# Two row maxima of a score burst taken one by one in a fused attention kernel

## The chip, the cores and the metric

The kernel runs on one core of a Trainium2 chip. The metric is the device time of one execution in microseconds (us); the kernel before takes 741.09 us (median of 3 runs, 741.09 to 741.41). In the text PE is TensorE (matmuls), PEld its weight loads, DVE is VectorE, ACT ScalarE, POOL GpSimd and SP the queue that issues most transfers. [...] The kernel holds PSUM, the memory that matmuls write to, as one tile of 128 partitions x 8 banks x 512 fp32 values.

## The reference

```
x: (8, 512, 512) fp32    cond: (8, 512)    16 heads of 32
Q = x @ Wq.T + bq ;  K = x @ Wk.T + bk ;  V = x @ Wv.T + bv
tQ = cond @ Wq.T + bq ;  tK = cond @ Wk.T + bk          # one row per batch
scores = (Q + tQ) @ (K + tK).T / sqrt(32)                # per batch and head, 512 x 512
out = x + softmax(scores) @ V
```

Everything is fp32. Four heads (4 x 32 = 128 columns) of one batch make a group; with 8 batches and 16 heads there are T = 32 groups, numbered t.

## The kernel before

The scores of a group are computed twice, once in each orientation. Once with the queries on the partitions: `row_max` (line 470) issues four matmuls through `row_scores` (line 481), one head each, for one chunk of 128 queries. Each head uses 32 of the array's 128 rows, so the four matmuls run side by side, and each fills one PSUM bank of 128 queries x 512 keys. Such a set of four is called a score burst here. From the four banks DVE takes the negated maximum over the keys (`row_max_of`, line 490, two banks per instruction), and ACT then takes exp(score - maximum) with the row sum as a by-product (`denominators`, line 518). The exponentials of that pass are thrown away, only the sums are kept. The profile shows line 518 as an ACTIVATE and a short ACTIVATION_READ_ACCUMULATOR for each head.

Once with the keys on the partitions: `exponentials` (line 555) first broadcasts the maxima of the group into four banks (line 560), adds the transposed scores to them (line 563), and ACT writes exp of each bank to SBUF (line 574). These tiles are the weights that `times_v` (line 579) multiplies by V.

The main loop over t has four stages for each t, one for each chunk, numbered 0 to 3 here. A stage issues, on PE in this order: the broadcasts of line 560, the transposed scores of line 563, the score burst of line 481 for the next group (`row_max(t + 1, 1)`, `(t + 1, 2)`, `(t + 1, 3)` and `(t + 2, 0)` in stages 0 to 3), and then a filler of its own: a part of the next batch's Q projection in stage 0, weights times V and its division in stage 1 (`weighted`), a part of the K projection in stage 2, a part of the V projection in stage 3. The projections use a seven-product scheme on 2 x 2 blocks; a t with odd number makes the first products of Q and K and a t with even number the other ones, for V it is the other way round. So the loop has eight kinds of stage. They are named E0 to E3 for even t and O0 to O3 for odd t.

The order on every engine is written out by hand. ACT does, in each stage: the four exponentials of line 574, then (O0, O2, E3 only) a copy of a first product (line 426), then the four discarded exponentials of line 518. DVE does the two maxima of line 490, then the sums that end the stage's projection: lines 432, 433 and 414 or 417 where the first products are made, lines 446, 447 and 414 or 417 for the others; in stage 3 a copy of the transposed maxima (line 550) stands between the maxima and these sums; in stage 1 it is a reciprocal (626), for two of four t two combinations of x (321 to 325), and a transpose (629).

All eight banks are in use all the time. A table `TURNS` gives, for each of the eight kinds, the bank of each use: entries 0 to 3 are the banks of the transposed scores (some of which the filler takes over afterwards), entries 4 to 7 those of the score burst. A weight load of a score burst therefore waits until the reader of its bank in the stage before is done: ACT's line 518 for banks that held scores, DVE's lines 414, 417, 447 or 629 for banks that held a product.

`row_max_pair` and `row_max_pairs` do the same as `row_max` for single pairs at the end of the program; the change does not touch them. `row_max` is called with its default pairs everywhere.

Of the kernel before, what the change touches and what calls it, by code (L numbers as in the profile page):

```python
# [12 lines left out]
ALU = mybir.AluOpType  # L13
AX = mybir.AxisListType
# [3 lines left out]
def kernel(  # L18
# [38 lines left out]
    nc = tc.nc  # L57
# [5 lines left out]
    HG = P // HD  # L63
    NP = HG // 2
# [42 lines left out]
    def banks(i, n=1):  # L107

        j = TURNS[turn[0]][i]
        if n == 1:  # L110
            return psum[:, j, :]
        k = TURNS[turn[0]][i + 1]
        return psum[:, j : k + 1 : k - j, :]
# [348 lines left out]
    nmax = {}  # L462
    sums = {}

    def open_max(t):
        if t not in nmax:
            nmax[t] = op.tile([P, NS, HG, 1], F32, tag="nmax", name=f"nmax_{t}", bufs=3)
            sums[t] = op.tile([P, NS, HG, 1], F32, tag="sums", name=f"sums_{t}", bufs=3)

    def row_max(t, qc, prs=range(NP)):  # L470
        if t >= T:
            return
        open_max(t)
        for j in range(HG):
            row_scores(t, qc, j, banks(HG + j))
        for pr in prs:
            row_max_of(t, qc, pr, banks(HG + pr * 2, 2))

    def row_scores(t, qc, j, pt):
        r = slice(j * HD, (j + 1) * HD)  # L480
        nc.tensor.matmul(  # L481
            pt,
            qkT["q", t][r, qc * P : (qc + 1) * P],
            qkT["k", t][r, :],
            start=True,
            stop=True,
        )

    def row_max_of(t, qc, pr, pt):
        nc.vector.tensor_reduce(  # L490
            nmax[t][:, qc, pr * 2 : pr * 2 + 2, 0], pt, AX.X, ALU.max, negate=True
        )
# [255 lines left out]

    turn[0] = 13
    row_max(0, 0)  # L750
    denominators(0, 0)
    project_qk(1, "k", banks(1))
    advance()
    row_max(0, 1)
    first_products("q", 0, 1, lambda: denominators(0, 1), nothing, 0, 1)
    advance()
    row_max(0, 2)
    other_products("q", 0, 1, lambda: denominators(0, 2), nothing, (0, 1))
    first_products("k", 0, 1, nothing, nothing, 3, 2)
# [94 lines left out]
    t = T - 3  # L854
# [36 lines left out]
    t = T - 2  # L891
# [101 lines left out]
```

## Time and profile before

| what | value |
|---|---|
| median of 3 runs | 741.09 us (741.09 to 741.41) |
| the profiled execution, whole | 741.09 us |
| its span, first to last instruction | 739.3 us |
| mean granted TensorE clock | 0.999 |
| PE busy | 730.4 us (99%) |
| ACT busy | 629.4 us (85%) |
| DVE busy | 523.4 us (71%) |
| POOL busy | 166.6 us (23%) |

The span leaves 1.8 us of the time outside it. Busy time counts an engine from the start to the modelled end of its instructions, and matmuls overlap: a busy PE can still be held up. In the tables a group of instructions is one line with its engine, operation, written and read tiles, shapes and count, then its busy time and the mean duration of one, then the engine's idle time before them and what ended it. In a timeline a row merges instructions of one line: start, time to the last end, count. Each fp32 matmul is two instructions in the trace, so a score burst is x8.

### The profile page before, as it was taken

Reading aid. Unit: us, or ns where it says so; the run is one execution under the profiler, and the core shown is the slowest. Engines: PE = TensorE matmul, PEld = TensorE weight load, DVE = VectorE, ACT = ScalarE, POOL = GpSimd, SP = SyncE. Lnnn points to the kernel's source line nnn. Section 1 sums busy time; section 2 is a strip of 40 time slices with the busy share of each in tenths; the row PEclk is TensorE's granted clock in tenths of the full one; section 3 lists DMA queues with packets and bytes.
Section 4 is the critical chain, followed back from the end, with each engine's and each line's share of the span. In section 5 each row is a group of like instructions: output and inputs, shape, how many; then the busy total and the mean of one; then the engine's idle time right before and its main releaser. Section 6 shows DMA issues by size and latency. Waiting matters only on the chain.

```text
span 739.3 us, 14941 instructions
## 1 busy us (share of the span) xinstructions
PE 730.4 (99%) x5434; PEld 407.5 (55%) x5434; DVE 523.4 (71%) x727; ACT 629.4 (85%) x1567; POOL 166.6 (23%) x270
## 2 busy tenths in 40 slices
PE   9999999999999999999999999999999999999997
PEld 5576555665555665555565555566555566555332
DVE  3588677777777776687766867777767777667664
ACT  2469889898998988989988988989889898898965
POOL 3721211222211222221122221122221122221130
PEclk9999999999999999999999999999999999999999
DMA  8512212222212222211212221222110111110111
GB/s 265 81 20 39 37 23 44 33 41 44 43 23 37 42 31 44 44 29 31 44 30 44 43 34 26 43 33 41 31 27 9 25 29 30 29 30 12 32 31 29
DMA packets 184765, 29.63 MB, mean 40 GB/s; under 512 B 178410, under 2 KB 182506, under 8 KB 184692
## 3 DMA queue, kind: packets, MB, share of 16 engines
q1 hardware_dynamic: 184112, 28.01, 22.0%
q8 instruction: 42, 0.69, 0.4%
q10 hardware_dynamic: 580, 0.68, 0.3%
q14 instruction: 31, 0.25, 0.1%
HBM read 20.27 MB, written 8.39 MB: 39 GB/s over the span
## 4 chain that ended last, share of the span: by engine, by line
PE 97%; ACT 1%; DMA 1%; DVE 1%; issue 0%; SPq 0%; DVEq 0%; ACTq 0%
PE psum L394 26%; PE psum L481 16%; PE psum L579 16%; PE psum L563 15%; PE psum L391 14%; PE psum L560 6%; PE psum L338 2%; PE psum L544 1%; DMA w_k<-in_L_cond_Wk_dram 1%; ACT e L574 1%; PE psum L254 1%; PE psum L638 0%; PE psum L589 0%; PE psum L677 0%; PE psum L618 0%
## 5 line engine op out<-in xcount | busy, mean ns | idle before, releaser
L490 DVE TENSOR_REDUCE nmax<-psum 128x2 f32<-128x1024 f32 x256 | 301.8, 1220 | 158.1 <-PE psum L481 156.6
L518 ACT ACTIVATE dead<-psum,nmax 128x512 f32<-128x512 f32 x496 | 334.8, 690 | 20.9 <-DVE nmax L490 17.6
L574 ACT ACTIVATE e<-psum 128x512 f32<-128x512 f32 x512 | 264.3, 602 | 59.6 <-PE psum L563 59.4
L481 PE MATMUL psum<-kT,qT 32*128 32x512 f32 x1024 | 142.0, 605 | 0.1
L563 PE MATMUL psum<-qT,kT 32*128 32x512 f32 x1024 | 132.4, 588 | 0.0
L630 POOL TENSOR_TENSOR res<-res,recs 128x512 f32<-128x512 f32 x28 | 29.4, 1049 | 438.5 <-DVE res L629 438.5
L579 PE MATMUL psum<-e,v 128*32 128x512 f32 x1024 | 120.3, 596 | 1.0 <-ACT e L574 0.9
L518 ACT ACTIVATION_READ_ACCUMULATOR dead<-psum,nmax 128x1 f32 x496 | 102.5, 207 | 0.0
L481 PEld LDWEIGHTS psum<-kT,qT 32*128 32x128 f32 x1024 | 58.7, 183 | 60.7 <-ACT dead L518 29.9
L579 PEld LDWEIGHTS psum<-e,v 128*32 128x32 f32 x1024 | 26.8, 110 | 65.9 <-issue 41.1
L560 PE MATMUL psum<-maxT,onesb 3*128 3x512 bf16 x512 | 51.3, 384 | 1.6 <-DVE maxT L550 0.9
L563 PEld LDWEIGHTS psum<-qT,kT 32*128 32x128 f32 x1024 | 51.1, 185 | 2.5 <-issue 0.2
L391 PE MATMUL psum<-wc_v,xc 128*128 128x256 f32 x192 | 49.3, 379 | 0.0
L560 PEld LDWEIGHTS <-onesb 3*128 3x128 bf16 x512 | 13.3, 91 | 60.4 <-issue 51.0
L394 PE MATMUL psum<-xc,wc_q 128*128 128x256 f32 x180 | 46.2, 379 | 0.0
L394 PE MATMUL psum<-xc,wc_k 128*128 128x256 f32 x180 | 46.2, 379 | 0.0
L391 PEld LDWEIGHTS psum<-wc_v,xc 128*128 128x128 f32 x192 | 36.5, 190 | 5.0
L391 PE MATMUL psum<-wT_v,xT 128*128 128x256 f32 x128 | 38.7, 404 | 0.0
L394 PEld LDWEIGHTS psum<-xc,wc_q 128*128 128x128 f32 x180 | 34.2, 190 | 4.7
L394 PEld LDWEIGHTS psum<-xc,wc_k 128*128 128x128 f32 x180 | 34.2, 190 | 4.6
L631 POOL TENSOR_TENSOR res<-res,xr 128x512 f32<-128x512 f32 x28 | 35.7, 1274 | 2.2
L170 POOL TENSOR_TENSOR xr<-xr,bvs 128x512 f32<-128x512 f32 x28 | 35.6, 1271 | 0.2 <-issue 0.2
(157 smaller groups left out, 739.2 us busy)
## 6 DMA issues: line engine op xcount, KB each, us to landing
x<-in_x_dram SPq DMA_DIRECT2D x112, 64.0 KB, 2.4
xr<-in_x_dram SPq DMA_DIRECT2D x112, 64.0 KB, 2.5
out_dram<-res SPq DMA_DIRECT2D x112, 64.0 KB, 2.0
w_q<-in_L_cond_Wq_dram SPq DMA_DIRECT2D x4, 256.0 KB, 4.5
w_k<-in_L_cond_Wk_dram SPq DMA_DIRECT2D x4, 256.0 KB, 3.8
w_v<-in_L_cond_Wv_dram SPq DMA_DIRECT2D x4, 256.0 KB, 4.3
xr<-in_x_dram SPq DMA_DIRECT2D x4, 256.0 KB, 4.0
out_dram<-res SPq DMA_DIRECT2D x3, 256.0 KB, 2.4
```

The lines of the kernel that those rows point to most:

```text
L170: nc.gpsimd.tensor_tensor(xr[t], xr[t], bias, ALU.add)
L391: nc.tensor.matmul(pt, xb, w, start=(kc == kcs[0]), stop=(kc == kcs[-1]))
L394: nc.tensor.matmul(pt, w, xb, start=(kc == kcs[0]), stop=(kc == kcs[-1]))
L481: nc.tensor.matmul(pt, qkT["q", t][r, qc * P : (qc + 1) * P], qkT["k", t][r, :], start=True, stop=True,)
L490: nc.vector.tensor_reduce(nmax[t][:, qc, pr * 2 : pr * 2 + 2, 0], pt, AX.X, ALU.max, negate=True)
L518: nc.scalar.activation(dead, banks(HG + j), AF.Exp, bias=nmax[t][:, qc, j, :], accum_out=sums[t][:, qc, j, :],)
L560: nc.tensor.matmul(bank[j], onesb[r, :], maxT[t][r, :], start=True, stop=False)
L563: nc.tensor.matmul(bank[j], qkT["k", t][r, kc * P : (kc + 1) * P], qkT["q", t][r, :], start=False, stop=True,)
L574: nc.scalar.activation(e[:, i, :], bank[pr * 2 + i], AF.Exp)
L579: nc.tensor.matmul(pt[j * HD : (j + 1) * HD, :], vs[b % 2][:, kc, (g * HG + j) * HD : (g * HG + j + 1) * HD], es[t, kc, j // 2][:, j % 2, ...
L630: nc.gpsimd.tensor_tensor(y, y, rec.broadcast_to([P, NB, BL]), ALU.mult)
L631: nc.gpsimd.tensor_tensor(y, y, xr.pop(t), ALU.add)
```

## The change

In `row_max` the maximum over banks HG and HG + 1 (heads 0 and 1), one instruction over 128 x 1024 values that writes 128 x 2, becomes two instructions over 128 x 512 values that write 128 x 1 each. The pair of heads 2 and 3 is taken as before. The argument `prs`, which no caller passes, is dropped. `row_max` is called for 31 groups and 4 chunks, 124 times; nothing else is edited, and no instruction of another engine is added, removed or moved. The four maxima of a burst stand in `nmax` as before.

```diff
-    def row_max(t, qc, prs=range(NP)):
+    def row_max(t, qc):
         if t >= T:
             return
         open_max(t)
         for j in range(HG):
             row_scores(t, qc, j, banks(HG + j))
-        for pr in prs:
-            row_max_of(t, qc, pr, banks(HG + pr * 2, 2))
+        for j in range(2):
+            nc.vector.tensor_reduce(
+                nmax[t][:, qc, j : j + 1, 0], banks(HG + j), AX.X, ALU.max, negate=True
+            )
+        row_max_of(t, qc, 1, banks(HG + 2, 2))
```

## The prediction

> **What bounds the kernel.** I read the page's busy times and groups first, then the list of waits, then single stages in the timeline. PE is busy throughout, and the chain that ended last is 97% PE, so time can only come from matmuls that are held up while they count as busy.
>
> ```profile
> PE 730.4 (99%) x5434; PEld 407.5 (55%) x5434; DVE 523.4 (71%) x727; ACT 629.4 (85%) x1567; POOL 166.6 (23%) x270
> ...
> L490 DVE TENSOR_REDUCE nmax<-psum 128x2 f32<-128x1024 f32 x256 | 301.8, 1220 | 158.1 <-PE psum L481 156.6
> L518 ACT ACTIVATE dead<-psum,nmax 128x512 f32<-128x512 f32 x496 | 334.8, 690 | 20.9 <-DVE nmax L490 17.6
> ```
>
> DVE's maxima wait for the burst, ACT's discarded exponentials wait 17.6 us in all for the maxima. The list of waits says who holds the burst's weight loads:
>
> ```profile
> PEld psum L481 <- ACT dead L518: 29.9, 77, 0.8
> ...
> ACT dead L518 <- DVE nmax L490: 17.6, 50, 5.0
> ...
> PEld psum L481 <- DVE qT L417: 11.2, 28, 0.9
> ...
> PEld psum L481 <- DVE v L414: 3.4, 14, 0.3
> ```
>
> A late load need not delay a matmul. How much it does is seen in PE's timeline, one pair of t (14, 15), the burst of each stage:
>
> ```profile
> 360.24 1.02 PE L481 MATMUL psum<-kT,qT 32*128 32x512 f32 x8
> ...
> 365.51 1.12 PE L481 MATMUL psum<-kT,qT 32*128 32x512 f32 x8
> ...
> 376.54 1.11 PE L481 MATMUL psum<-kT,qT 32*128 32x512 f32 x8
> ...
> 387.44 1.11 PE L481 MATMUL psum<-kT,qT 32*128 32x512 f32 x8
> ...
> 398.47 1.14 PE L481 MATMUL psum<-kT,qT 32*128 32x512 f32 x8
> ```
>
> E0 (360.24) is undisturbed at 1.02, as are E2, O0 and O2; E1 (365.51), E3, O1 and O3 are stretched. In the trace's single records the step from a burst's first matmul to the filler's first is 954 ns undisturbed, 1,045 in E1, 1,041 in E3, 1,044 in O1 and 1,064 in O3, almost the same in every pair, while every other piece of a stage is constant to 2 ns. So the late loads cost 91 + 87 + 90 + 110 = 378 ns a pair, 5.3 us over 14 pairs. That is the most that this change could give in the loop.
>
> The records also show the rule. Counted from the start of line 563, a burst's first matmuls can start at 862 ns; a head's second load comes 108 ns after its first, and its second matmul 427 ns after that load, but not before 1,290 to 1,301. So a first load is free until about 756 to 765 ns and costs one for one after that. A load follows the release by some 43 to 52 ns.
>
> **The change, part by part.**
>
> *DVE's work.* One reduction of 1024 becomes two of 512. No row shows 512, but the program has a reduction of 128 values from PSUM: 281 ns, against 1,214 for 1024 (1,224 where it waited). The line through them is 1.041 ns per value, which puts 512 at 681 (691). Back to back, DVE starts the next instruction 84 ns before the end of the last: the two reductions of a stage take 2.36 us together, so the second starts 1.14 after the first. The two halves thus occupy 607 + 597 = 1,204 ns instead of 1,141: 63 ns more in each of 124 bursts, 7.8 us of DVE, which has 29% to spare but not everywhere.
>
> *Start.* Today the pair waits for both heads. The trace's semaphore updates show PE's completions posted about 43 ns apart (1,890 and 1,933 after line 563's start in E0), and the reduction starts at 1,957, 24 after the second. Alone, head 0 can start at 1,914. In E0 to E3, O2 and O3 the maxima therefore begin 43 ns sooner. DVE's shift for what follows is s = 63 - 43 = 20 ns.
>
> *ACT.* This is the stage before E1, with the ACT and DVE rows:
>
> ```profile
> 361.34 2.36 DVE L490 TENSOR_REDUCE nmax<-psum 128x2 f32<-128x1024 f32 x2 [1.27 <-PE psum L481]
> ...
> 362.66 0.69 ACT L518 ACTIVATE dead<-psum,nmax 128x512 f32<-128x512 f32 x1 [0.16 <-DVE nmax L490]
> ...
> 363.61 0.41 DVE L446 TENSOR_TENSOR qT<-psum,qT 128x256 f32<-128x256 f32 x1
> ...
> 363.94 0.68 DVE L447 TENSOR_TENSOR qT<-psum,qT 128x512 f32<-128x512 f32 x1
> ...
> 364.58 0.75 DVE L417 SCALAR_TENSOR_TENSOR qT<-psum,tok,qT 128x512 f32<-128x512 f32 x1
> ```
>
> The first maxima end at 361.34 + 1.22 = 362.56, and line 518 starts 95 ns later; ACT issued its last exponential at 361.89 and, at its pitch of 0.48 to 0.49, was free at 362.37. So ACT loses 0.29 us here. After the change head 0's maximum ends at 361.30 + 0.69 = 361.99, and ACT starts at 362.37. Head 1 follows at 363.05. Head 2 waits for the pair, which ends 20 ns later than today: 363.71 + 0.095 = 363.81, against 364.00 now. ACT's last two heads come 190 ns sooner. E1's loads wait for them (the last ends at 798 ns and the load is at 850); at 608 the load is free, and the 88 ns are gone. E1's other gate is DVE's line 417 (load at 737, free until 756), fed by the back-to-back rows 446 and 447. Line 417 waits for PE's last product anyway, with 42 ns to spare over the pitch of 447, so s = 20 costs nothing: **-88 ns in E1**.
>
> E3 has the same relief on ACT, but its first load follows line 417, whose K it needs: 686 ns end, 802 load. Line 417 has the same 42 ns to spare: **0 in E3**. O3 follows O2, where a copy (line 426) keeps ACT until 3,254 ns and the maxima until 3,277: **-22 in O3**. O1 follows O0, where the copy alone sets the start at 3,254: **0 in O1**. E0 waits for line 414, at the end of a back-to-back chain from O3's maxima (2.36 us, then lines 550, 446, 447, 414), load at 736 and 15 ns to spare to the last head: **+5 in E0**. E2 waits for the transpose of line 629, which follows PE's last weighted product; in every other pair two combinations of x before it leave it 74 ns. The earlier PE takes 88 and s takes 20, so it is 34 late, less some 20 of room at the load: **+15 in half of E2**. PE's filler, the wait of line 618 on the second exponential included, has room for E1's 88.
>
> Sum: 14 x (-88 - 22 + 5) = -1.47, E2 +0.10, t = 26 whose E1 is stretched by half only +0.04, the first stages -0.03, the end of the program -0.2 (there the maxima hold ACT for 0.37 and 0.18, and its bursts are stretched by 0.3 and 0.1, of which 0.13 and 0.07 come back). Together -1.6 us, against the profiled execution's 741.09 (739.3 of span and 1.8 around it), which is also the median: **739.5 us**. POOL and the transfers get the maxima of the last chunk 20 ns later; line 544 waits for POOL's end over 1 us later, so nothing follows.
>
> [...] The row says that a second reduction costs 157 ns of fixed time (1,224 less 1,024 values at 1.04), of which 84 are covered: some 63 to 73. [...]
>
> **The rivals.** (a) Forecast, 739.5, own range 738.9 to 740.2. (b) The early start isn't had or the second reduction costs more: s = 40 to 85, E1's relief and the dearer E0 and E3 about cancel. [...] For it: three of four gates of the even stages are DVE chains with 15 to 42 ns to spare. Against: the postings 43 ns apart. (c) Slower: DVE's back-to-back chains become the bound of E0, E1 and E3. [...] For it: PE's slack there is a few tens of ns. Against: the interpolated 63. (d) More: E3's first load is at 802 though its DVE release was at 697; if the rest is ACT's, E3's 87 go too, 14 x 87 = 1.2 us, 738.3. Against: that load needs a separate wait instruction, which the trace shows. That nothing happens isn't a case: three maxima in place of two are issued.
>
> **How the numbers follow.** (a) 0.48, (b) 0.21, (c) 0.19, (d) 0.12. What a measurement can tell from no change is 0.2%, 1.5 us; 739.6 is the line, and six tenths of (a) lie below it. Faster: 0.29 + 0.12 = 0.41. Same: 0.19 + 0.21 = 0.40. Slower: 0.19. The range is 738.3 (d) to 743.0, most of (c).
>
> **What would show it.** 124 reductions of 1024 fewer, 248 of 512 with 680 to 690 ns; DVE's busy time up 8 us; ACT's wait for line 490 from 17.6 to under 8 us; E1's burst at 1.03 instead of 1.12, O3's at 1.12 instead of 1.14, E0's still 1.02. Wrong is the forecast if the halves take over 710 ns, if the first one starts no sooner after the burst, or if E0's or E3's burst grows by more than 0.03.

## The result

The changed kernel takes 739.41 us (median of 13 runs, 739.18 to 740.33) against 741.09 us (13 runs beside it, 740.73 to 742.37): a ratio of 0.9978, 95% interval 0.9969 to 0.9986. The forecast was 739.5. The profiled spans are 737.5 us after and 739.3 before. In the changed kernel lines from `row_max` on have numbers that are higher by 3: the single maxima are line 477, the pair 493, the burst 484, the discarded exponentials 521.

The page of the changed kernel, busy times and groups:

```profile
PE 729.1 (99%) x5434; PEld 406.9 (55%) x5434; DVE 529.9 (72%) x851; ACT 626.4 (85%) x1567; POOL 166.2 (23%) x270
...
L521 ACT ACTIVATE dead<-psum,nmax 128x512 f32<-128x512 f32 x496 | 338.0, 701 | 8.3 <-DVE nmax L477 5.4
...
L477 DVE TENSOR_REDUCE nmax<-psum 128x1 f32<-128x512 f32 x248 | 159.7, 686 | 149.5 <-PE psum L484 149.5
L493 DVE TENSOR_REDUCE nmax<-psum 128x2 f32<-128x1024 f32 x132 | 160.2, 1214 | 2.8 <-PE psum L484 2.8
```

The 248 halves take 686 ns each, and ACT loses 8.3 us ahead of its discarded exponentials where it lost 20.9. Its mean of 701 instead of 690 comes back below. In the list of waits, of the changed kernel (what waits, for what: us in all, times, longest):

```profile
PEld psum L484 <- ACT dead L521: 26.8, 60, 1.0
...
PEld psum L484 <- DVE qT L417: 11.1, 28, 0.5
...
ACT dead L521 <- DVE nmax L477: 5.4, 2, 4.5
...
PEld psum L484 <- DVE v L414: 3.3, 14, 0.2
```

ACT waited 50 times for maxima, 17.6 us in all; it now waits five times, 6.3 us in all (the two of the row, and three for the pair of line 493), all in the first 52 us. The burst's loads wait for ACT 60 times instead of 77, and for DVE as before. DVE's busy time is up by 6.5 us where 8 was named. The timeline of PE, changed kernel, t = 14 and 15, the bursts of E0, E1, E3, O1 and O3:

```profile
359.75 1.03 PE L484 MATMUL psum<-kT,qT 32*128 32x512 f32 x8
...
365.02 1.02 PE L484 MATMUL psum<-kT,qT 32*128 32x512 f32 x8
...
375.96 1.11 PE L484 MATMUL psum<-kT,qT 32*128 32x512 f32 x8
...
386.86 1.20 PE L484 MATMUL psum<-kT,qT 32*128 32x512 f32 x8
...
397.98 1.13 PE L484 MATMUL psum<-kT,qT 32*128 32x512 f32 x8
```

E1's burst has lost its stretch (1.12 to 1.02); E3's and O3's have not. O1's 1.20 is a single stage: in other pairs it is 1.10 to 1.11. It will be explained by the last experiments. DVE and ACT in stage E0, just ahead of E1:

```profile
360.80 1.29 DVE L477 TENSOR_REDUCE nmax<-psum 128x1 f32<-128x512 f32 x2 [1.21 <-PE psum L484]
...
361.86 0.71 ACT L521 ACTIVATE dead<-psum,nmax 128x512 f32<-128x512 f32 x1
362.00 1.21 DVE L493 TENSOR_REDUCE nmax<-psum 128x2 f32<-128x1024 f32 x1
...
364.09 0.75 DVE L417 SCALAR_TENSOR_TENSOR qT<-psum,tok,qT 128x512 f32<-128x512 f32 x1
```

The first maximum starts 1.05 us after the burst's first matmul (before 1.10), and ACT goes on at 361.86 with no idle time in its row, 2.11 us after the burst started (before 2.42). Line 417 still comes 4.34 after the burst, as it did: DVE's longer work cost E1's other gate nothing. In the records of E1 at t = 14, the last two of the heads' first loads started 850 and 856 ns after the start of line 563 (566 now); they now start at 753 and 759, within the 756 to 765 up to which a load is free.

A pair is the eight stages of two successive t. In the single records the whole difference of 1.81 us in span is found: 1.11 in the 13.5 pairs from t = 1 to 27 (43.876 us a pair before, 43.794 after, with stages that are stretched only once left out), 0.30 in such one-off stages (0.76 us before, 0.46 after), 0.13 ahead of t = 1 and 0.30 behind t = 27; the sum is 1.84. Not all of it is the change's. A second execution of the changed kernel starts t = 1 0.09 us later than the first, so the 0.13 is not shown to be an effect. What O1 and O3 give, 11 ns a pair, comes back below.

### The profile page after: what moved, and what is told of

The parts are those of the page before. It is cut to its first block, busy times and chain, and to the rows that moved or that the text cites. A ratio compares the mean times of both kernels' runs of the same rounds, so it can differ in the third digit from the quotient of the medians.

```text
span 737.5 us, 15136 instructions
## 1 busy us (share of the span) xinstructions
PE 729.1 (99%) x5434; PEld 406.9 (55%) x5434; DVE 529.9 (72%) x851; ACT 626.4 (85%) x1567; POOL 166.2 (23%) x270
## 4 chain that ended last, share of the span: by engine, by line
PE 97%; DVE 1%; ACT 1%; DMA 0%; issue 0%; DVEq 0%
PE psum L394 26%; PE psum L582 16%; PE psum L484 15%; PE psum L566 15%; PE psum L391 14%; PE psum L563 6%; PE psum L338 2%; PE psum L547 1%; ACT e L577 1%; PE psum L254 1%; DMA x<-in_x_dram 0%; PE psum L299 0%; PE psum L641 0%; DVE nmax L477 0%; PE psum L592 0%; PE psum L680 0%
## 5 line engine op out<-in xcount | busy, mean ns | idle before, releaser
L477 DVE TENSOR_REDUCE nmax<-psum 128x1 f32<-128x512 f32 x248 | 159.7, 686 | 149.5 <-PE psum L484 149.5
L493 DVE TENSOR_REDUCE nmax<-psum 128x2 f32<-128x1024 f32 x132 | 160.2, 1214 | 2.8 <-PE psum L484 2.8
L484 PE MATMUL psum<-kT,qT 32*128 32x512 f32 x1024 | 140.3, 602 | 0.2 <-DVE kT L417 0.2
L521 ACT ACTIVATION_READ_ACCUMULATOR dead<-psum,nmax 128x1 f32 x496 | 108.6, 219 | 0.0
L484 PEld LDWEIGHTS psum<-kT,qT 32*128 32x128 f32 x1024 | 56.7, 183 | 61.0 <-ACT dead L521 26.8
```

The lines of the kernel that those rows point to most:

```text
L477: nc.vector.tensor_reduce(nmax[t][:, qc, j : j + 1, 0], banks(HG + j), AX.X, ALU.max, negate=True)
L484: nc.tensor.matmul(pt, qkT["q", t][r, qc * P : (qc + 1) * P], qkT["k", t][r, :], start=True, stop=True,)
L493: nc.vector.tensor_reduce(nmax[t][:, qc, pr * 2 : pr * 2 + 2, 0], pt, AX.X, ALU.max, negate=True)
L521: nc.scalar.activation(dead, banks(HG + j), AF.Exp, bias=nmax[t][:, qc, j, :], accum_out=sums[t][:, qc, j, :],)
```

## The experiments

The table has, from the records of each profiled execution, the median step in ns from a burst's first matmul to the filler's first (954 to 956 is undisturbed), and the mean pair in us without stages that are stretched once.

| kernel | E0 | E1 | E2 | E3 | O1 | O3 | pair, us | median, us |
|---|---|---|---|---|---|---|---|---|
| before | 956 | 1046 | 955 | 1041 | 1044 | 1064 | 43.876 | 741.09 |
| changed | 962 | 955 | 965 | 1042 | 1038 | 1059 | 43.794 | 739.41 |
| split in E0 only | 956 | 956 | 956 | 1041 | 1036 | 1058 | 43.778 | 738.93 |
| split in all but E0 | 965 | 1034 | 954 | 1042 | 1037 | 1058 | 43.869 | 740.44 |
| head 1 first | 1008 | 1063 | 956 | 1116 | 1075 | 1071 | 44.113 | 745.11 |
| heads 2, 3 singly | 1008 | 998 | 964 | 1046 | 1038 | 1057 | 43.887 | 740.85 |
| all four singly | 1029 | 956 | 995 | 1056 | 1044 | 1064 | 43.920 | 740.54 |
| split in E0, O2, ends | 956 | 954 | 956 | 1042 | 1044 | 1065 | 43.794 | 739.01 |

Some entries stand between two kinds that alternate from one even t to the next: E2 for the changed kernel (955 and 974), with heads 2, 3 singly (955 and 973) and with all four singly (955 and about 1,038), and E3 for the last two (1,040 and 1,055; 1,041 and 1,071).

### The split in E0 alone, and everywhere else

The edit is to the changed kernel, like the next ones:

```diff
+        single = t % 2 == 1 and qc == 1 and t > 1   # the burst that stage E0 issues
-        for j in range(2):
+        for j in range(2) if single else ():
             nc.vector.tensor_reduce(...)
-        row_max_of(t, qc, 1, banks(HG + 2, 2))
+        for pr in (1,) if single else (0, 1):
+            row_max_of(t, qc, pr, banks(HG + pr * 2, 2))
```

> The maxima of heads 0 and 1 are taken singly in stage E0 alone (14 bursts), together everywhere else. Theory (the gain is ACT's earlier start in E0, which frees the banks that E1's burst loads wait for): E1's step from the burst's first matmul to the filler falls from 1,046 to 955 ns, every other stage stays as before the change (E0 956, E3 1,041, O1 1,044, O3 1,064), E2 goes up by at most 20 in every other pair; 14 x 90 = -1.26, +0.1: 739.9 us, ratio 0.9984. Rival (the gain comes from many stages, or from the maxima starting sooner everywhere): a seventh or less of the change's 1.7 us, 740.8. Rival (the gain is one run's hiccups): E1 stays at 1,046 and the time at 741.1.

Measured: 738.93 us (7 runs), ratio 0.9974, interval 0.9963 to 0.9986. The other way round, the split in all bursts but those (`single = not (t % 2 == 1 and qc == 1)`):

> Heads 0 and 1 singly everywhere but in E0. Theory: E1 stays at 1,046 ns; E0 pays 7 (from O3's maxima), O3 and O1 gain 5 each, E2 has no earlier filler to catch up with, so it stays at 955; the start and the end of the program give 0.25 us. Together about 0.3 us below before: 740.8, ratio 0.9996. Rival (many stages give a little each): most of the 1.7 us stays, 739.6.

Measured: 740.44 us, ratio 0.9994, interval 0.9985 to 1.0003; it is 0.36 below the expected time, and its one-off stretch is 0.06 us where before had 0.76. So 14 of 124 bursts carry all of the gain in the loop: the pair loses 98 ns with them alone, 91 of them in E1, and 7 with all the others. The split of O3's maxima costs E0 its 9 ns (965 against 956). E0 alone was 1.0 us better than expected, of which 0.76 is that this execution has no one-off stretched stage at all.

O1 and O3 read 6 to 8 ns below before in the kernel that leaves their stages alone. In all traces but that of head 1 first they have one of two pairs of values: about 1,037 and 1,058 in six (the changed kernel twice, E0 alone, all but E0, heads 2 and 3, and a kernel below with memsets), 1,044 and 1,064 in seven (before, all four singly, the split in E0, O2 and the ends, and four kernels with memsets, one of them the changed kernel). So these 11 to 13 ns a pair, some 0.15 us in all, go neither with the split nor with its absence. What decides them stays open.

### Head 1 ahead of head 0

```diff
-        for j in range(2):
+        for j in (1, 0):
```

> The two single maxima of the changed kernel in the other order, head 1 and then head 0: the same instructions, but ACT's first discarded exponential needs the second of them. Theory (head 0's earliness is all that is bought): head 0's maximum ends at about 1,957 + 607 + 681 = 3,246 ns after line 563's start, against 3,182 with one instruction for both, so ACT starts 65 later than before the change in E0, E1, O2 and about 87 later in O0; bursts E1 +65, O3 +65, O1 +87 against before, E0 +48 and E3 +21 by VectorE's longer chains: +286 ns a pair, 4.0 us: 745.1, ratio 1.0054. Rival (splitting as such helps, whatever the order): 739.4 to 740.

Measured: 745.11 us (4 runs), ratio 1.0057, interval 1.0043 to 1.0071. The total is as expected, its parts are not: the pair grows by 237 ns and not by 286, E1 by 17 for 65, O1 by 31 for 87, E3 by 75 for 21. The same two instructions as in the changed kernel, and it is slower than before. In its timeline of PE, the bursts of E0, E1 and E3 of t = 14:

```profile
362.05 1.08 PE L484 MATMUL psum<-kT,qT 32*128 32x512 f32 x8
...
367.36 1.22 PE L484 MATMUL psum<-kT,qT 32*128 32x512 f32 x8
...
378.50 1.18 PE L484 MATMUL psum<-kT,qT 32*128 32x512 f32 x8
```

E0 pays here for DVE's second reduction without the early start, with 1,008 ns for 956. The 1.22 in E1 is one-off in this pair; its median is 1,063 ns, above before's 1,046, since in E0 ACT's first discarded exponential starts 71 ns later than before and not 300 sooner. That E1 pays only 17 of the 71 fits E0's own 52, by which E1 begins later; the next experiment shows this. So the gain is the early release of head 0, and the order is what gives it.

### The other pair, and all four, singly

```diff
-        for j in range(2):
+        row_max_of(t, qc, 0, banks(HG, 2))
+        for j in (2, 3):
             nc.vector.tensor_reduce(...)
-        row_max_of(t, qc, 1, banks(HG + 2, 2))
```

> Heads 0 and 1 together as before, heads 2 and 3 one by one: the same added VectorE work, without an earlier head 0. Theory: VectorE's chain is 63 ns later (607 + 597 in place of 1,141), ACT gains nothing; E0 +48, E1 +0 (ACT's late load hides VectorE's), E3 +21, others 0: +69 ns a pair, 1.0 us: 742.1, ratio 1.0013. Rival (VectorE's 63 ns are hidden by its idle quarter): 741.1, no stage changed. Rival (splitting as such helps): 739.5.

Measured: 740.85 us, ratio 0.9997, interval 0.9988 to 1.0006: no slower, where 1.0013 was expected. With all four heads singly (`for j in range(HG)`, no pair):

> All four maxima of a burst singly. ACT gets all four heads in time (head 2 no longer waits for a pair), VectorE's chain is 126 - 43 = 83 ns later than before the change. Theory: E1's gate is now VectorE's line 417, 41 late, so its burst falls only from 1,046 to about 990; E0 +68, E3 +41, O3 -5, E2 +23 on the mean of two: +70 ns a pair, 1.0 us, end of the program -0.1: 742.0, ratio 1.0012; that would show that VectorE's few tens of ns of room are the limit of this kind of change. Rival (more splitting, more relief): below 739.4.

Measured: 740.54 us, ratio 0.9993, interval 0.9984 to 1.0002; 1.0012 was expected. Both came out lower than expected. The timeline of PE of the kernel with heads 2 and 3 singly, E0 and E1 of t = 14:

```profile
360.30 1.08 PE L484 MATMUL psum<-kT,qT 32*128 32x512 f32 x8
365.61 1.07 PE L484 MATMUL psum<-kT,qT 32*128 32x512 f32 x8
```

E0 pays (1,008 ns, +52; +48 was expected), but E1 falls by 48 although nothing releases ACT earlier: its first exponential still starts 3,282 ns after line 566's start, 3,276 before. That start hangs on matmuls ahead of the stall. When E0's burst is stretched by 52, the next stage begins 52 later, and E1's gates stand 52 earlier against it. So a stall in E0 takes the place of the one in E1, and the pair grows by 11 ns, not by 69: 58 ns in each of 14 pairs, 0.8 of the 1.25 us by which the time is below the expected one (13 of the 58 are O1's and O3's). Most of the rest is that its one-off stretched stages come to 0.38 us and not 0.76.

With all four singly E0 pays 73 (68 expected), and E1 is free (956) where DVE's later line 417 was to keep it at 990. E2 pays 80 in half of the pairs, 40 on the mean for 23, and E3 15 on the mean for 41: it pays 30 where E2 is free, and nothing where E2 pays. The pair grows by 44 ns where 70 was expected, 0.4 of the 1.46 us by which the time is below the expected one. Another 0.63 is in one-off stages, 0.1 at the ends of the program; the rest lies between the profiled execution (740.89) and the median.

### The split where it can pay, and the changed kernel beside it

The loops are those of the split in E0 alone; only the choice differs:

```diff
+        single = (
+            (t % 2 == 1 and qc == 1) or (t % 2 == 0 and qc == 3)
+            or t in (0, T - 2) or (t == 1 and qc == 0)
+        )
```

> Heads 0 and 1 singly only where a later burst waits for ACT: E0, O2, and in the first and the last groups. Theory: the change's gain in E1 and O3 and at both ends stays, its costs go: E0 back from 962 to 955, E2 from 975 to 965 in every other pair (the part that the earlier filler causes stays): 14 x 7 + 7 x 10 = 0.17 us below the changed kernel, 739.2 against 739.4, ratio to before 0.9975. Rival (the other splits matter): slower than the changed kernel by 0.2 or more.

> The changed kernel itself, on the same chip as the version that splits only in chosen stages. 739.4, ratio to before 0.9978; E1 955, E0 962, E2 965 on the mean, E3 1,042, O1 1,038, O3 1,059 ns.

Measured: 739.01 us, ratio 0.997, interval 0.996 to 0.9981, against 739.42 us, 0.997 to 0.9988, for the changed kernel on the same chip. O3 reads 1,065 with the maxima of O2 split, for which it waits, just as before (1,064): the gain that was forecast for O3 isn't there. E0 and E2 are back at 956, E2 in every pair, where 965 was expected in every other one.

### The stages that are stretched once

The kernel before has three: t = 11 O0 by 224 ns, t = 22 E1 by 254 and t = 26 E0 by 280. The changed kernel has two, t = 2 E3 by 373 and t = 15 O1 by 88, and a second execution of it has the same two, by 355 and 103. In each, one instruction ahead of it began late. Timeline of DVE, kernel before, ahead of t = 22 E1:

```profile
539.46 0.68 DVE L447 TENSOR_TENSOR qT<-psum,qT 128x512 f32<-128x512 f32 x1
540.46 0.75 DVE L417 SCALAR_TENSOR_TENSOR qT<-psum,tok,qT 128x512 f32<-128x512 f32 x1 [0.31 <-ACT dead L518]
```

Line 417 follows 447 by 0.62 to 0.64 us elsewhere, and by 1.00 here. The row names ACT as releaser, but the records have line 417's separate wait instruction end at 540.06, 0.40 us ahead of it, where 0.05 is usual. The same row in the changed kernel, ahead of t = 2 E3:

```profile
111.28 0.68 DVE L447 TENSOR_TENSOR kT<-psum,kT 128x512 f32<-128x512 f32 x1
112.27 0.75 DVE L417 SCALAR_TENSOR_TENSOR kT<-psum,tok,kT 128x512 f32<-128x512 f32 x1 [0.31 <-DVE kT L447]
```

Counted through DVE's records, the separate wait instructions too, the late ones before are numbers 448, 832 and 960, and this one is 192: all multiples of 64. If the count decides, instructions put ahead of the loop move the stretched stages. The experiment is a few memsets of a column that nobody reads:

```diff
     nc.vector.memset(which, 0.0)
+    pad = const.tile([P, 1], F32, tag="pad", name="pad")
+    for _ in range(4):      # 4, 6 or 5 in the kernel before, 9 in the changed one
+        nc.vector.memset(pad, 0.0)
```

> The kernel before, with four one-element-wide memsets more at the head of DVE's program, long before the loop. Theory: DVE pauses at every 64th of its instructions (separate wait instructions counted; a gap of about 0.48 us where it follows a wait instruction of a chain without idle time), and the kernel before loses 224 + 254 + 280 = 758 ns where this falls into such a chain, in the stages at 293, 540 and 623 us. Four instructions more move every pause four instructions earlier in the program, where by the trace of before none meets line 414, 417 or 490 in a chain of the loop that a burst waits for. Expected: no stage stretched by over 0.1 us in the loop, 740.3 us, ratio 0.999. Rival (the stretched stages come from transfers or from something else fixed in time): the same three stages stretched, 741.1, ratio 1.000.

Measured: 740.41 us, ratio 0.9991, interval 0.9982 to 0.9999. The stretches at t = 11 and t = 22 are gone. At t = 26 E0 one of 203 remains, but from another instruction: number 960 is now the copy of line 550, at the head of the chain to line 414, which I hadn't counted among the chains. DVE ahead of t = 22 E1, with four memsets more (447 and 417 stand in lines 450 and 420):

```profile
539.59 0.68 DVE L450 TENSOR_TENSOR qT<-psum,qT 128x512 f32<-128x512 f32 x1
540.23 0.75 DVE L420 SCALAR_TENSOR_TENSOR qT<-psum,tok,qT 128x512 f32<-128x512 f32 x1
```

Six memsets:

> The kernel before, with six such memsets. Theory: the three pauses leave t = 11, 22 and 26, and others reach line 490 of t = 6 E3 (stage t = 7 O0 stretched by 0.22 us), line 417 of t = 18 E0 (t = 18 E1 by 0.25) and line 414 ahead of t = 24 E0 (by 0.28): 741.1 us, ratio 1.000, but the stretched stages are those. Rival: those of before, t = 11 O0, 22 E1 and 26 E0.

Measured: 741.05 us, ratio 0.9999, interval 0.999 to 1.0008. Stretched are t = 7 O0 by 219 ns and t = 18 E1 by 254, where and as much as expected, and none of the old ones; t = 24 E0, the third that was expected, is not. DVE ahead of t = 18 E1:

```profile
451.63 0.68 DVE L450 TENSOR_TENSOR qT<-psum,qT 128x512 f32<-128x512 f32 x1
452.62 0.75 DVE L420 SCALAR_TENSOR_TENSOR qT<-psum,tok,qT 128x512 f32<-128x512 f32 x1 [0.31 <-ACT dead L521]
```

The changed kernel with nine:

> The changed kernel with nine such memsets. Theory: the pauses of t = 2 E3 and t = 15 O1 go and no other falls into a chain that a burst waits for: 0.46 us less than the changed kernel, 738.95 us, ratio 0.9971 to the kernel before. Rival: 739.4, ratio 0.9978, with the stretched stages where they were.

Measured: 739.38 us, ratio 0.9977, interval 0.9968 to 0.9987: a miss. t = 2 E3 is undisturbed, but t = 15 O1 is stretched by 88 as before, and t = 19 O2 by 323, since number 832 is now the transpose (line 629 before) of t = 19, which I hadn't counted either. The 88 of t = 15 is ACT's. Its rows in the changed kernel:

```profile
384.66 0.70 ACT L521 ACTIVATE dead<-psum,nmax 128x512 f32<-128x512 f32 x1
385.23 0.23 ACT L521 ACTIVATION_READ_ACCUMULATOR dead<-psum,nmax 128x1 f32 x1
385.44 0.69 ACT L521 ACTIVATE dead<-psum,nmax 128x512 f32<-128x512 f32 x1
```

The ACTIVATE at 385.44 follows the last one by 0.78, where 0.67 is usual, and is number 1,088, 17 x 64, of ACT's records. Memsets on DVE don't move it. Next, the selective split with five memsets:

> The kernel with the maxima split in E0 and O2 and in the first and last groups only, with five such memsets. Theory: the pause ahead of t = 14 E0 goes (0.29 us) and with it the 0.05 at t = 11 O3: 738.7 us, ratio 0.9968. Rival: 739.0, ratio 0.9973.

Measured: 738.62 us (5 runs), ratio 0.9965, interval 0.9952 to 0.9979, the lowest time of the study and below both kernels, though its interval reaches into the changed kernel's. The 285 ns at t = 14 E0 are gone; the 0.05 at t = 11 O3 stays: it is ACT's, its late ACTIVATE being number 832 of ACT's records.

What the six memsets missed at t = 24 settles the period. Line 414 there was number 896, 14 x 64; every instruction that came late had an odd multiple. Five memsets in the kernel before leave no chain of a waited-for burst at odd multiples and three at even ones:

> The kernel before with five memsets more at the head of DVE's program. In all traces so far the pauses stand only at the odd multiples of 64 in the count of an engine's instructions (64, 192, 320 and so on: once in 128), never at the even ones. Theory (once in 128): no pause reaches a chain of the loop that a burst waits for, no stage is stretched by over 0.03 us, 740.3 us, ratio 0.999. Rival (once in 64): pauses at line 417 of t = 8 E2 and t = 20 E0 and at line 550 of t = 27 O3, so t = 8 E3 and t = 20 E1 are stretched by 0.25 us: 740.9.

Measured: 740.33 us (11 runs), ratio 0.9989, interval 0.998 to 0.9998. No stage of the loop is stretched. Line 417 ahead of t = 20 E1 is number 768, 12 x 64, and follows 447 by 0.63:

```profile
495.19 0.68 DVE L450 TENSOR_TENSOR qT<-psum,qT 128x512 f32<-128x512 f32 x1
495.82 0.75 DVE L420 SCALAR_TENSOR_TENSOR qT<-psum,tok,qT 128x512 f32<-128x512 f32 x1
```

The kernel before thus gets 0.7 us faster by five memsets of which no result is used.

## Why the prediction was right, and where not

**E1, the 88 ns: right.** Predicted -88, measured -91, 14 times; the run with E0 alone shows that this is the gain, and the run with head 1 first that it hangs on the early release of head 0. The early start of 43 ns was had to the nanosecond: the first maximum of E0 to E2 begins 1,914 ns after the scores' start, 1,956 before.

**The second reduction's price: right.** The halves occupy 608 and 597 to 598 ns (607 and 597 forecast), and the pair behind them ends 20 ns later (4,333 against 4,313): s is 20. The trace shows 64 to 65 ns more for the second reduction (608 and 597 to 598 against 1,141), since the next one starts 82 to 84 ns before the last one's end; the estimate from the row of 1,024 values was 63 to 73.

**E0, E2 and E3: right.** E0 +6 (forecast +5); E2 +20 in half of the pairs (+15), and none where E1's maxima are taken in pairs (E0 alone, 956), so s is what it pays; E3 0, 1,042 against 1,041. That refutes rival (d), which had E3's 87 go with ACT's relief: E2's heads do end earlier and E3's first load does not.

**O3, the step that failed: -22 forecast, about 0 measured.** The step said that ACT, which waits until 3,277 for the maxima in O2, is free at 3,254 by the copy, so the last head comes 22 sooner. The first exponential does start at 3,252 instead of 3,276. But each ACTIVATE then takes 713 instead of 690 ns, and the last head doesn't end sooner for it: it ends 796 to 797 ns into the next stage, or 802 to 804, in four and three traces with O2's maxima split, and in two and four with O2's as before. The 5 ns by which O3 reads lower are this difference, which the kernel with O2 untouched has too (E0 alone, 1,058) and the changed kernel with nine memsets has not (1,064). In O0, where the copy always set the start, the ACTIVATE had 714 before the change too. What holds the last head's end stays open. The step was worth 0.31 us in the sum.

**The one-off stages, which no step had: -0.30.** The 124 instructions added to DVE, and 70 more separate wait instructions on ACT (2,031 records before, 2,101 after; the edit adds none there itself), move the late ones to other places: 0.76 us of stretch became 0.46. This is chance, and made up for O3. Without the stretches the kernel before takes 740.33 (measured), and the changed kernel 739.41 - 0.46 = 738.95 (argued, since nine memsets met another chain), 1.4 us less. Of these, 0.15 are O1's and O3's lower values, so the change itself is worth some 1.2 to 1.4 us, not 1.7. The forecast of 739.5 was nearer than its parts: the loop gave 1.11 where 14 x (-88 - 22 + 5) and the terms for E2 and t = 26 made 1.33, the two ends 0.43 where 0.23 was forecast, the stretches 0.30 where nothing was. Of the ends, 0.2 to 0.3 behind t = 27 are clear: from there to the end of the span it is 72.16 to 72.27 us in the four traces of the kernel before, with memsets or without, and 71.87 to 71.99 in the three of the changed one.

**Rivals (b) and (c): the terms don't stand alone.** They didn't happen because s is 20. The upper end of the range, 743.0, needs a dearer second reduction than the 64 to 65 ns of the changed kernel; no run shows one. Added up by stages, E0 pays s - 15, E1 s - 50 less its 88, E3 s - 42, and O3 keeps 22: 3s - 217 ns a pair. The 50 was the author's estimate, and the sum takes each stage's loss as independent. With heads 2 and 3 singly it isn't: E0's 52 take 48 from E1's stall. With all four singly DVE's pair ends 85 ns later (4,398 against 4,313), and the formula's 3 x 85 - 217 = +38 meets the measured +44, but by a loss in E2 that it hasn't and without the one in E1 that it has.

## What to carry to other kernels

Split an instruction where a waiting engine can start on the first half, and only there: here 14 of 124 places gave all that the loop gained, and others cost a little. Before adding up stalls of neighbouring stages, ask which gate hangs on work ahead of the first stall: that one gets the stall as slack (here E0's 52 ns took 48 from E1's). When two kernels differ by a few tenths of a per cent, compare the typical stage first, and look at the single stages that stand out: here four to nine memsets moved those that were DVE's.

## What was not expected of the hardware

**An instruction stream that pauses once in 128 instructions.** Over the loops of the 14 traces of this case, DVE instructions that directly follow a wait instruction, with a usual gap under 0.3 us, came 0.12 to 0.37 us late in 20 of the 23 cases where their number was an odd multiple of 64, and never by more than 3 ns in the 24 cases where it was an even one. Each of the 20 started 0.40 to 0.44 us after its wait instruction's end, whatever the usual gap is. The three without delay are one place in three traces: number 704, line 493 of t = 16 E1, behind the wait instruction of the transpose. Three ACT instructions ahead of stretched stages, numbers 832, 960 and 1,088, came 0.08 to 0.12 late. The places go with the program: the two executions of the changed kernel have the same ones.

The traces have a hint at what the engine does there. The page of the kernel before has a DMA queue that moves instructions (packets, MB, share of the DMA engines' time):

```profile
q14 instruction: 31, 0.25, 0.1%
```

In the records these 31 packets have 8,192 bytes each. In all 20 late cases such a packet begins 0.65 to 1.26 us after the late instruction has started; for DVE's numbers from 101 to 1,050 that are no multiple of 64, one begins 0.5 to 1.3 us after the start in 5% of cases, and in the kernel before none begins within 1.5 us of an even multiple of 64. So the pause goes with such a packet. It isn't a wait for that packet, which begins later; what the engine does in that time was not shown.

**An ACTIVATE's record can lengthen with the work unchanged.** 690 ns where it waited for a maximum, 713 in O2 after the change, and 722 in E0 with all four heads singly. In O2 start plus duration stayed within 5 ns of the old sum. Durations of such rows are no measure of a gain here; ends are.
